# Down projection by Strassen's seven products for three of four pairs of token tiles

## The chip, the cores and the metric

The kernel runs on one core of a Trainium2 chip. A core has TensorE (PE, matrix products), VectorE (DVE), ScalarE (ACT), GpSimd (POOL) and SyncE (SP, which here only issues transfers). Each engine works through its own queue in order; semaphores hold an instruction until what it needs is there. The metric is the time of one execution on the device in microseconds (us). Before the change the median of three runs is 322.97 us (322.59 to 323.91).

## The reference

The input is x, 1024 tokens of width 512; everything is float32.

```
xn  = layernorm(x)
s   = silu(xn @ w_gate.T)                     # 1024 x 1376
s   = s with the 688 smallest |s| of each row set to 0
s   = s * (xn @ w_up.T)
ffn = routed experts (top 2 of 16, grouped) + shared expert, on xn
out = x + (s @ w_down.T) * silu(ffn)          # 1024 x 512
```

The change bears on the last line: the down projection `s @ w_down.T` (inner length 1376), the product with the gate `silu(ffn)`, the sum with x, and the store.

## The kernel before

**Tiles and pairs.** The 1024 tokens are eight tiles of 128. Tiles j and j+4 form pair j (`NP` = 4 pairs). `S[t]` is the tile's row of s, 128 x 1392 floats in SBUF. The gate and up projections and the experts' first layers are already done by Strassen's scheme with seven half-size products (class `Unit`, lines 652 to 700): products m1 to m7 are accumulated in three PSUM tiles, `al`, `be` and `de`; after m1, m6 and m5 ScalarE copies `al` to SBUF (`copy`, lines 658 to 661: m, u, v), and m6, m5, m3 go on adding to the same `al`. The four output quarters come from `de + m`, `al`, `be + v` and, after m4 is added to `be`, `be + u`. `weight_sums` (line 644) forms the sums of the weights' blocks, one subtraction for each of t1, t2, t4 and the new b12.

**Order.** The kernel is compiled with a manual schedule: the order in which the Python code issues instructions is the order on each engine's queue. A main loop over slots (lines 1341 to 1352) issues the products of gate, shared experts, up and routed experts. Between them a `Filler` (line 1136) issues the steps of the search for each row's threshold, one generator for each pair (`search`, line 820, before it `absolute`, line 811). One search makes five rounds of two counts on ScalarE (line 841) and seven small POOL operations (lines 852 to 858); then for each of its two tiles a last count, a masking of the row (line 866) and a maximum of eight (line 869) on VectorE; then nine small VectorE operations (lines 871 to 888) and for each tile one that drops the small values in `S[t]` (line 892). At the end of the main loop, pairs 0 and 1 have been through the search, pair 2 has done four of its five rounds, pair 3 two.

**The last stage** (from line 1354) is where the change is made. Tiles are handled in the order 0, 4, 1, 5, 2, 6, 3, 7 (`tiles`).

- `experts_base(i)` (line 1316): VectorE writes the biases of the experts for tile i into `y[t]`, two operations of 512 elements. `place` is the list of buffers for y; before, three lie in a retired weight buffer and three in the buffers t1, t2, t4 (`more_y`).
- `experts(i)` (line 1326, `experts_out` line 1088): TensorE makes three products into three PSUM tiles (`pys`, `pyr` twice); VectorE adds each to y (lines 1095, 1099); at the end ScalarE applies silu (line 1101), which gives the gate. After each of the three, the filler may be asked for steps.
- `turn_product(t, sT)` (line 1104): TensorE transposes the eleven chunks of `S[t]` (the last is 96 wide) in three groups, each with its own PSUM tile; ScalarE copies them to `sT` (lines 1113, 1119).
- `finish` (line 1121): eleven matmuls of width 512, `sT` against `wd_sb`, accumulate in one PSUM tile `po`; VectorE multiplies by the gate (line 1130), POOL adds x (line 1132), SP issues the store (line 1133). The last tile is done in two halves of 256 columns, with VectorE for the sum.

Before, the order is: experts of the first four tiles, turning of the first, and then for each tile the turning of the next, finish, and the experts of the tile four ahead.

**PSUM and SBUF.** All PSUM tiles come from one pool with one tag and eight banks (line 516); a new tile gets a bank whose former tile has been read. `wd_sb` is loaded at the end of the main loop into the buffer that the up weights leave (line 1355). The tiles of x are loaded a second time (`again`, four buffers).

Of the kernel before, what the change touches and what calls it, by code (L numbers as in the profile page):

```python
# [9 lines left out]
F32 = mybir.dt.float32  # L10
# [43 lines left out]
PERIOD = 7  # L54

# [434 lines left out]
def quick_path(  # L490
# [597 lines left out]
    def experts_out(t, g, ex):  # L1088
        def down_expert(name, which):
            py = psum(f"py{name}{t}")  # L1090
            mul_acc(py, [(h[:, ts(t, P)], w) for w, h in which], True)
            return py

        py = down_expert("s", ex[:2])
        nc.vector.tensor_add(g, g, py)
        yield
        for j, (gs, b3r) in enumerate(mix):
            py = down_expert(f"r{j}", ex[2 + j : 3 + j])
            nc.vector.scalar_tensor_tensor(g, py, gs[:, t : t + 1], g, ALU.mult, ALU.add)
            yield  # L1100
        nc.scalar.activation(g, g, AF.Silu)
# [19 lines left out]
    def finish(t, g, sT, xt, pieces=1):  # L1121
        for k in range(pieces):
            cols = ts(k, H // pieces)
            po = psum(f"po{t}_{k}")[:, : H // pieces]
            terms = []
            for c in range(IC):
                w = min(P, I - c * P)
                terms.append((sT[:w, c, :], wd_sb[:w, c, cols]))
            mul_acc(po, terms, True)
            nc.vector.tensor_mul(g[:, cols], po, g[:, cols])  # L1130
            add = nc.gpsimd if pieces == 1 else nc.vector
            add.tensor_tensor(g[:, cols], g[:, cols], xt[:, cols], ALU.add)  # L1132
            nc.sync.dma_start(out[ts(t, P), cols], g[:, cols])
# [92 lines left out]
    routed, hid, w3, b3s, du = [], [], [], [], {}  # L1226
# [66 lines left out]
    def fetch_w3():  # L1293
        w = w12("w3")
        for i in range(SLOTS):
            w3.append(w[:, ts(i, H)])
            fetch(w3[2 + i], w_rows, slots[i][0])
        b3s.append(w[:, 2 * H : 3 * H])
        nc.sync.dma_start(b3s[0], b3[E].partition_broadcast(P))
# [6 lines left out]
    ahead = 4  # L1306
# [5 lines left out]
    def more_y():  # L1312
        for k in ("t1", "t2", "t4"):
            place.append(big.tile([P, GW], F32, tag=k, name=f"{k}y")[:, :H])

    def experts_base(i):
        t = tiles[i]
        y[t] = place[i % 6]
# [9 lines left out]

    at(r_at + 20, begin_y)
# [3 lines left out]

    def search_job(j):
        yield from absolute(j)
        yield from search(j)

# [16 lines left out]
    more_y()  # L1354
    wd_sb = big.tile([P, IC * H], F32, tag="wB", name="wd_sb").rearrange("p (c n) -> p c n", c=IC)
    full = I // P
    for c0, c1 in ((0, 4), (4, 8), (8, full)):
# [3 lines left out]
    nc.sync.dma_start(wd_sb[: I - full * P, full, :], wd[full * P :, :])  # L1361
# [3 lines left out]
        for i in range(5)  # L1365
    ]
    for i in range(ahead):
        for _ in experts(i):
            filler.draw(0.3)
        if i + 3 < 6:  # L1370
            experts_base(i + 3)
    turn_product(tiles[0], sT[0])
    for i, t in enumerate(tiles):
        if i + 1 < NT:
            turn_product(tiles[i + 1], sT[(i + 1) % len(sT)])
        if i + 3 < NT:
            again[tiles[i + 3]] = load_x(tiles[i + 3], "r")
        finish(t, y[t], sT[i % len(sT)], again[t], pieces=2 if i == NT - 1 else 1)
        if i + ahead < NT:
            for _ in experts(i + ahead):  # L1380
                filler.draw(3)
            if i + 6 < NT:
                experts_base(i + 6)

        if i == NT - 4:
            filler.rest()
            worst = small.tile([P, 1], F32, tag="worst", name="worst")
            nc.vector.tensor_reduce(worst, bad, AX.X, ALU.add)
        if i == NT - 2:
            pf = psum("pf")  # L1390
            nc.tensor.matmul(pf[:1, :1], worst, ones[:, 0:1], start=True, stop=True)
            nc.vector.tensor_single_scalar(flag[:1, :], pf[:1, :1], 0.0, ALU.is_gt)

# [88 lines left out]
```

## Time and profile before

| | |
|---|---|
| median of three runs | 322.97 us (322.59 to 323.91) |
| the profiled execution's own time | 322.64 us |
| its span, from the first to the last recorded instruction | 320.8 us |
| granted TensorE clock, mean | 0.992 of full speed |
| `po` (down projection) on TensorE | 198 records, 77.1 us busy |
| line 841 (counts) on ScalarE | 40 + 8 records of 1.44 us |
| last stage on TensorE | from 200.5 to 314.7 us |

How to read what is shown further on. The busy table gives, for each engine, busy time, share of the span and number of instructions; PEld is the loading of a matmul's stationary operand, which overlaps PE. A line of a timeline gives the start, the duration, the engine, the source line, the operation, output<-inputs, the shape and the number of instructions merged; in brackets stands the idle time ahead of it and who ended it. Matmuls are pipelined and their ends are modelled, so starts are surer than ends. The line number 704 is that of the helper that issues all matmuls of a product; the PSUM tile's name tells which it is. A line of the chain gives start, duration, and what the end of the kernel was waiting for then. A line of the table by stretches gives from:to, its length, the busy time of PE, PEld, DVE, ACT and POOL, each with a count, then PEclk (granted TensorE clock as a share of full speed), the DMA engines' share and GB/s.

### The profile page before, as it was taken

How to read it: one execution, taken by the hardware profiler on the slowest of the kernel's cores; microseconds unless marked ns; L12 is line 12 of the kernel's file. 1: busy time of each engine (PE TensorE's matmuls, PEld its weight loads, DVE VectorE, ACT ScalarE, POOL GpSimd, SP SyncE). 2: the span in 40 equal slices, each digit the busy share in tenths (PEclk: the TensorE clock that was granted, in tenths of full speed). 3: DMA queues.
4: the chain of work that ended last, by engine and by line, in shares of the span. 5: the costliest groups of instructions: out<-in, count | busy, mean ns of one | idle time of the engine just before them, and what ended most of it. 6: DMA issues, size and time to landing. Idle time of an engine off the chain costs nothing.

```text
span 320.8 us, 3076 instructions
## 1 busy us (share of the span) xinstructions
PE 306.3 (95%) x964; PEld 172.8 (54%) x964; DVE 178.8 (56%) x384; ACT 148.4 (46%) x248; POOL 105.2 (33%) x229
## 2 busy tenths in 40 slices
PE   7899999999999997999999997999999999999992
PEld 3566566666544564654456664454545454555481
DVE  5988943323488671499399642790357889100011
ACT  2224556662983853637767567535181432211000
POOL 3242110112395078815532766400404020011010
PEclk9999999999999999799999999999999999999999
DMA  7992000000100006000070000910201020200010
GB/s 212 372 415 109 0 0 0 2 1 0 66 0 3 0 3 185 8 0 0 4 194 1 1 3 0 337 47 0 67 0 65 0 65 0 67 33 0 33 54 22
DMA packets 9735, 19.01 MB, mean 59 GB/s; under 512 B 1376, under 2 KB 3728, under 8 KB 9712
## 3 DMA queue, kind: packets, MB, share of 16 engines
q1 hardware_dynamic: 8976, 16.62, 15.2%
q0 software_dynamic: 736, 2.13, 2.5%
q8 instruction: 9, 0.15, 0.2%
q14 instruction: 14, 0.11, 0.1%
HBM read 16.65 MB, written 2.10 MB: 58 GB/s over the span
## 4 chain that ended last, share of the span: by engine, by line
PE 75%; DVE 10%; POOL 4%; ACT 4%; issue 2%; DMA 2%; SPq 0%; DVEq 0%; POOLq 0%
PE po L704 24%; PE palg L704 8%; PE palu L704 7%; PE pz L704 5%; PE pals L704 4%; PE pbeg L704 4%; PE pbeu L704 3%; PE palr L704 3%; PE pyr L704 3%; PE pys L704 3%; DMA wg_sb<-in_wg_dram 2%; PE ps L1111 2%; PE pdeg L704 2%; PE pbes L704 2%; ACT j L841 2%
## 5 line engine op out<-in xcount | busy, mean ns | idle before, releaser
L704 PE MATMUL po<-wd_sb,sT 128*128 128x512 f32 (+3 forms) x198 | 77.1, 546 | 0.7 <-ACT sT L1113 0.7
L841 ACT ACTIVATE j<-a,c 128x1376 bf16<-128x1376 f32 x40 | 57.7, 1443 | 24.4 <-POOL c L858 22.4
L704 PEld LDWEIGHTS po<-wd_sb,sT 128*128 128x128 f32 (+1 forms) x198 | 37.0, 190 | 35.6 <-issue 33.5
L704 PE MATMUL palu<-wu_sb,xs 128*128 128x344 f32 x64 | 22.4, 474 | 1.8 <-ACT vu L660 1.8
L1130 DVE TENSOR_TENSOR w_y<-po,w_y 128x512 f32<-128x512 f32 (+1 forms) x6 | 3.6, 602 | 33.6 <-PE po L704 33.6
L1132 POOL TENSOR_TENSOR w_y<-w_y,xr 128x512 f32<-128x512 f32 x4 | 5.1, 1268 | 51.0 <-DVE w_y L1130 41.6
L704 PE MATMUL pz<-wg_sb,xs 128*128 128x348 f32 x64 | 19.9, 461 | 1.4 <-ACT xs L630 0.9
L1113 ACT COPY sT<-ps 128x512 f32<-128x512 f32 (+1 forms) x24 | 10.7, 518 | 16.8 <-PE ps L1111 16.8
L1035 POOL TENSOR_TENSOR s<-s,vu 128x344 f32<-128x344 f32 x8 | 10.0, 1250 | 24.8 <-DVE vu L1034 24.7
L704 PEld LDWEIGHTS palu<-wu_sb,xs 128*128 128x128 f32 x64 | 12.7, 199 | 9.5 <-ACT vu L660 2.3
L704 PEld LDWEIGHTS pz<-wg_sb,xs 128*128 128x128 f32 x64 | 11.8, 190 | 8.2 <-ACT xs L630 1.5
L704 PE MATMUL palg<-wg_sb,xs 128*128 128x348 f32 x48 | 16.0, 456 | 0.0
L866 DVE SCALAR_TENSOR_TENSOR w<-a,c 128x1376 f32<-128x1376 f32 x8 | 13.8, 1722 | 2.3 <-POOL c L858 2.3
L704 PE MATMUL pys<-moe 128*128 128x512 f32 x32 | 15.0, 592 | 0.0
L704 PE MATMUL pyr<-w_w,moe 128*128 128x512 f32 x32 | 15.0, 592 | 0.0
L704 PE MATMUL palr<-xs,w_r 128*128 128x512 f32 x32 | 14.7, 592 | 0.0
L704 PE MATMUL pals<-xs,w_s 128*128 128x512 f32 x32 | 14.7, 592 | 0.0
L841 ACT ACTIVATE jc<-a,c 128x1376 bf16<-128x1376 f32 x8 | 11.5, 1443 | 4.9 <-POOL c L858 4.7
L892 DVE SCALAR_TENSOR_TENSOR s<-a,thr,s 128x1376 f32<-128x1376 f32 x8 | 13.1, 1644 | 0.0
L704 PE MATMUL palu<-t1u,xs 128*128 128x344 f32 x32 | 11.2, 474 | 1.9 <-ACT uu L660 1.9
L869 DVE MAX8 v<-w 128x8 f32<-128x1376 f32 x8 | 12.8, 1595 | 0.3
L1111 PEld LDWEIGHTS ps<-ident,s 128*128 128x128 f32 (+1 forms) x88 | 9.9, 139 | 3.7 <-issue 2.7
(230 smaller groups left out, 546.4 us busy)
## 6 DMA issues: line engine op xcount, KB each, us to landing
wu_sb<-in_wu_dram SPq DMA_DIRECT2D x4, 688.0 KB, 9.2
wg_sb<-in_wg_dram SPq DMA_DIRECT2D x3, 696.0 KB, 7.4
x<-in_x_dram SPq DMA_DIRECT2D x8, 256.0 KB, 4.0
xr<-in_x_dram SPq DMA_DIRECT2D x8, 256.0 KB, 4.6
wd_sb<-in_wd_dram SPq DMA_DIRECT2D x2, 1024.0 KB, 6.6
w_s<-in_wexp_dram SPq DMA_DIRECT2D x2, 512.0 KB, 5.4
out_dram<-w_y SPq DMA_DIRECT2D x4, 256.0 KB, 2.1
wg_sb<-in_wg_dram SPq DMA_DIRECT2D x1, 664.0 KB, 9.5
```

The lines of the kernel that those rows point to most:

```text
L704: nc.tensor.matmul(acc, a, b, start=first and i == 0, stop=i == len(terms) - 1, skip_group_check=not first,)
L841: nc.scalar.activation(junk, a[i], AF.Sign, bias=c[:, i : i + 1], scale=-1.0, accum_out=to[:, i : i + 1])
L866: nc.vector.scalar_tensor_tensor(w, a[i], c[:, i : i + 1], a[i], ALU.is_lt, ALU.mult)
L869: nc.vector.max(v[:, i, :], w)
L892: nc.vector.scalar_tensor_tensor(s, a[i], thr[:, i : i + 1], s, ALU.is_gt, ALU.mult)
L1035: nc.gpsimd.tensor_tensor(s, s, part, ALU.mult)
L1111: nc.tensor.transpose(pt[:w, ts(c - c0, P)], s[:, c * P : c * P + w], ident)
L1113: nc.scalar.copy(sT[:, c0 : c0 + full, :], pt[:, : full * P].rearrange("p (c n) -> p c n", c=full),)
L1130: nc.vector.tensor_mul(g[:, cols], po, g[:, cols])
L1132: add.tensor_tensor(g[:, cols], g[:, cols], xt[:, cols], ALU.add)
```

## The change

Pair 0 keeps `finish` for each of its two tiles, now without halves. Pairs 1, 2 and 3 go through a new class `Down(Unit)`: the two tiles' turned rows are a 2 x 2 block matrix (two tiles by two groups of `CH` = 5 chunks), the weights another (two groups of five chunks by two halves of 256 columns), and seven products of five matmuls of width 256 take the place of two times eleven of width 512. The last 96 rows of the inner length are added as one more matmul in each of m7, m2, m3 and m4; m4's takes the difference of the two halves of the weights' rows (`xw["diff"]`).

- The weights' sums t1, t2, t4 and the difference are formed by POOL after the turning of tile 0; b12, which pair 0 still needs in its old form, is replaced by VectorE after the second finish.
- The four sums of the rows (`sums`) are formed by VectorE in the buffers `S[j]` and `S[j + NP]` of the pair, which are free once turned.
- Each output quarter is `acc * g + (part * g + x)`: POOL prepares `part * g + x`, VectorE multiplies and adds, SP stores 128 x 256. The quarter out12 has no part, its second term is x.
- y's buffers are three of before, then four halves in `S[0]` and `S[4]`, then the first again. ScalarE's silu is no longer in `experts_out` but in `gate_of`.
- The order of the last stage is written out; the filler's steps are asked for by `some(n)`, and `turn_pair(j)` makes sure that pair j's search is complete.

```diff
+CH = 5
+LAST = I % P
             nc.vector.scalar_tensor_tensor(g, py, gs[:, t : t + 1], g, ALU.mult, ALU.add)
             yield
-        nc.scalar.activation(g, g, AF.Silu)
+    def finish(t, g, sT, xt):
+        po = psum(f"po{t}")
+        terms = []
+        for c in range(IC):
+            w = min(P, I - c * P)
+            terms.append((sT[:w, c, :], wd_sb[:w, c, :]))
+        mul_acc(po, terms, True)
+        nc.vector.tensor_mul(g, po, g)
+        nc.gpsimd.tensor_tensor(g, g, xt, ALU.add)
+        nc.sync.dma_start(out[ts(t, P), :], g)
+    class Down(Unit):
+        n = H // 2
+        def __init__(self, j, sT, gs, xts):
+            self.name, self.j, self.g, self.x = f"d{j}", j, gs, xts
+            top, bot = sT
+            s, k = S[j], CH * P
+            self.a = {
+                A11: top[:, :CH, :], A12: top[:, CH : 2 * CH, :],
+                A21: bot[:, :CH, :], A22: bot[:, CH : 2 * CH, :],
+            }
+            for blk, v in ((S1, S[j][:, :k]), (S2, S[j][:, k : 2 * k]), (S4, S[j + NP][:, :k])):
+                self.a[blk] = v.rearrange("p (c n) -> p c n", c=CH)
+            self.xtop, self.xbot = (v[:LAST, 2 * CH, :] for v in sT)
+        def sums(self):
+            a = self.a
+            nc.vector.tensor_add(a[S1], a[A21], a[A22])
+            nc.vector.tensor_sub(a[S2], a[S1], a[A11])
+            nc.vector.tensor_sub(a[A21], a[A11], a[A21])
+            nc.vector.tensor_sub(a[S4], a[A12], a[S2])
+        def mm(self, acc, blk, key, first, extra=()):
+            terms = [(self.a[blk][:, c, :], dd[key][:, c, :]) for c in range(CH)]
+            mul_acc(acc, terms + list(extra), first)
+        def m7(self):
+            self.be = self.acc("be")
+            self.mm(self.be, S3, "b12", True, [(self.xbot, xw["right"])])
+        def m2(self):
+            self.de = self.acc("de")
+            self.mm(self.de, A12, "b21", True, [(self.xtop, xw["left"])])
+            self.out11()
+        def m3(self):
+            self.mm(self.al, S4, "b22", False, [(self.xtop, xw["right"])])
+            self.out12()
+        def m4(self):
+            self.mm(self.be, A22, "t4", False, [(self.xbot, xw["diff"])])
+            self.out21()
+        def prepare_part(self, i, cols, part):
+            nc.gpsimd.tensor_tensor(part, part, self.g[i][:, cols], ALU.mult)
+            nc.gpsimd.tensor_tensor(part, part, self.x[i][:, cols], ALU.add)
+        def give(self, i, k, acc, part):
+            t, cols = self.j + NP * i, ts(k, H // 2)
+            g = self.g[i][:, cols]
+            nc.vector.tensor_mul(g, acc, g)
+            nc.vector.tensor_add(g, g, part)
+            nc.sync.dma_start(out[ts(t, P), cols], g)
+        def out11(self):
+            self.prepare_part(0, ts(0, H // 2), self.m)
+            self.give(0, 0, self.de, self.m)
+        def out12(self):
+            self.give(0, 1, self.al, self.x[0][:, H // 2 :])
+        def out22(self):
+            self.prepare_part(1, ts(1, H // 2), self.v)
+            self.give(1, 1, self.be, self.v)
+        def out21(self):
+            self.prepare_part(1, ts(0, H // 2), self.u)
+            self.give(1, 0, self.be, self.u)
...
-    def more_y():
-        for k in ("t1", "t2", "t4"):
-            place.append(big.tile([P, GW], F32, tag=k, name=f"{k}y")[:, :H])
...
+    def gate_of(i):
+        nc.scalar.activation(y[tiles[i]], y[tiles[i]], AF.Silu)
...
+    half = H // 2
+    dd = {
+        "b11": wd_sb[:, :CH, :half], "b12": wd_sb[:, :CH, half:],
+        "b21": wd_sb[:, CH : 2 * CH, :half], "b22": wd_sb[:, CH : 2 * CH, half:],
+    }
+    for k in ("t1", "t2", "t4"):
+        dd[k] = big.tile([P, GW], F32, tag=k, name=f"{k}d")[:, : CH * half].rearrange(
+            "p (c n) -> p c n", c=CH
+        )
+    xw = {"left": wd_sb[:LAST, full, :half], "right": wd_sb[:LAST, full, half:]}
+    xw["diff"] = spare[0][:LAST, :]
     flat = big.tile([P, 7, 2, HALF], F32, tag="xs", name="sT").rearrange("p b c n -> p (b c n)")
     sT = [
         flat[:, i * IC * P : (i + 1) * IC * P].rearrange("p (c n) -> p c n", c=IC)
-        for i in range(5)
+        for i in range(4)
     ]
-    for i in range(ahead):
+    def turn_pair(j):
+        while j not in found:
+            filler.one()
+        return [lambda k=k: turn_product(j + NP * k, sT[2 * (j % 2) + k]) for k in range(2)]
+    def unit_for(j):
+        return Down(
+            j, [sT[2 * (j % 2) + k] for k in range(2)],
+            [y[j + NP * k] for k in range(2)], [again[j + NP * k] for k in range(2)],
+        )
+    def some(n):
+        for _ in range(n):
+            filler.one()
+    for i in range(3):
         for _ in experts(i):
-            filler.draw(0.3)
-        if i + 3 < 6:
-            experts_base(i + 3)
-    turn_product(tiles[0], sT[0])
-    for i, t in enumerate(tiles):
-        if i + 1 < NT:
-            turn_product(tiles[i + 1], sT[(i + 1) % len(sT)])
-        if i + 3 < NT:
-            again[tiles[i + 3]] = load_x(tiles[i + 3], "r")
-        finish(t, y[t], sT[i % len(sT)], again[t], pieces=2 if i == NT - 1 else 1)
-        if i + ahead < NT:
-            for _ in experts(i + ahead):
-                filler.draw(3)
-            if i + 6 < NT:
-                experts_base(i + 6)
-        if i == NT - 4:
-            filler.rest()
-            worst = small.tile([P, 1], F32, tag="worst", name="worst")
-            nc.vector.tensor_reduce(worst, bad, AX.X, ALU.add)
-        if i == NT - 2:
+            some(1)
+        gate_of(i)
+    first = turn_pair(0)
+    first[0]()
+    weight_sums(G, *(dd[k] for k in KEYS), upto=3)
+    G.tensor_sub(xw["diff"], xw["left"], xw["right"])
+    place += [S[0][:, :H], S[0][:, H : 2 * H]]
+    experts_base(3)
+    some(4)
+    first[1]()
+    some(4)
+    place += [S[NP][:, :H], S[NP][:, H : 2 * H], place[0]]
+    finish(tiles[0], y[tiles[0]], sT[0], again[tiles[0]])
+    again[tiles[3]] = load_x(tiles[3], "r")
+    for _ in experts(3):
+        some(1)
+    for turn_one in turn_pair(1):
+        turn_one()
+    gate_of(3)
+    unit = unit_for(1)
+    unit.sums()
+    some(4)
+    finish(tiles[1], y[tiles[1]], sT[1], again[tiles[1]])
+    weight_sums(V, *(dd[k] for k in KEYS), since=3)
+    experts_base(4)
+    for j in range(1, NP):
+        more = j + 1 < NP
+        u, e = unit, 2 * j + 2
+        u.m1()
+        u.m7()
+        if j > 1:
+            gate_of(e - 1)
+        if more:
+            for i in (e, e + 1):
+                again[tiles[i]] = load_x(tiles[i], "r")
+        u.m6()
+        if more:
+            for _ in experts(e):
+                some(1)
+            experts_base(e + 1)
+            turns = turn_pair(j + 1)
+            turns[0]()
+            gate_of(e)
+        u.m2()
+        some(1)
+        u.m5()
+        if more:
+            some(1)
+            turns[1]()
+        else:
             pf = psum("pf")
             nc.tensor.matmul(pf[:1, :1], worst, ones[:, 0:1], start=True, stop=True)
             nc.vector.tensor_single_scalar(flag[:1, :], pf[:1, :1], 0.0, ALU.is_gt)
+        u.c22()
+        u.m3()
+        if more:
+            unit = unit_for(j + 1)
+            unit.sums()
+            for _ in experts(e + 1):
+                some(2)
+            if e + 2 < NT:
+                experts_base(e + 2)
+            else:
+                filler.rest()
+                worst = small.tile([P, 1], F32, tag="worst", name="worst")
+                nc.vector.tensor_reduce(worst, bad, AX.X, ALU.add)
+        u.m4()
```

## The prediction

> **What bounds the kernel now.** I read three views first: the busy table, TensorE's timeline from 200 us on, and the end of the chain that ended last.
>
> ```profile
> PE 306.3 (95%) x964; PEld 172.8 (54%) x964; DVE 178.8 (56%) x384; ACT 148.4 (46%) x248; POOL 105.2 (33%) x229
> ```
>
> ```profile
> 214.26 2.57 PE L1111 MATMUL ps<-ident,s 128*128 128x128 f32 x22
> 217.52 9.71 PE L704 MATMUL po<-wd_sb,sT 128*128 128x512 f32 x22 [0.69 <-ACT sT L1113]
> 227.07 1.88 PE L704 MATMUL pys<-moe 128*128 128x512 f32 x4
> 228.79 1.88 PE L704 MATMUL pyr<-w_w,moe 128*128 128x512 f32 x4
> 230.51 1.36 PE L1111 MATMUL ps<-ident,s 128*128 128x128 f32 x11
> 231.71 9.61 PE L704 MATMUL po<-wd_sb,sT 128*128 128x512 f32 x22
> ...
> 304.91 9.77 PE L704 MATMUL po<-wd_sb,sT 128*128 128x256 f32 x44
> ```
>
> ```profile
> 304.98 9.71 PE po L704 x44
> 314.69 0.02 issue
> 314.72 0.44 DVE w_y L1130
> ```
>
> TensorE sets the end: from 200.5 to 314.69 us it stands still only 0.69 us, ahead of the first down product. Starts give the prices, since an end overlaps the next start: a down product costs 9.45 us (231.71 to 241.16), the expert products of a tile 3.44 (227.07 to 230.51), the turning of a tile 1.20. An f32 matmul has two records here. At width 512 one record takes 9.45/22 = 0.43 us; at width 256, from the chain, 9.71 less 0.17 for the last one's way out, over 44: 0.217 us. Half the width is half the price. After TensorE's end come 0.44 + 0.42 us of VectorE and 5.2 us of the last store and the close.
>
> **What TensorE saves.** A pair had two down products, 18.90 us. It now has seven products of five chunks at width 256, 35 matmuls, and four matmuls for the 96 last rows: 39 x 2 x 0.217 = 16.9 us. Three pairs save 6.0. The 0.69 us ahead of the first down product goes: that wait came from ScalarE's gate of the fourth tile (line 1101), and experts(3) now comes after finish. TensorE's list without waits, from 200.53: three experts 10.30, two turnings 2.40, finish 9.45, experts 3.44, two turnings 2.40, finish 9.45, three pairs 50.8, four experts 13.75, four turnings 4.80, the flag's matmul 0.12, last way out 0.17. It ends at 307.6: **7.1 us** less.
>
> **What is added elsewhere, without waits.** POOL: three subtractions of 1280 elements. 344 elements take 0.915 us (line 1035) and 688 take 1.65 (line 647), so 2.14 ns each and 0.18 once: 2.92 us each, and 0.73 for "diff". VectorE: one such subtraction for b12 and four of 640 elements a pair. Its line 647 takes 0.42 us at 256 and 0.88 at 696: 1.48 and 0.82 us. The output quarters are two VectorE operations of 0.42 each (the last store's row) where one of 0.69 stood, and mostly two POOL operations of 0.73 where one of 1.27 stood. Three ScalarE copies a pair, some 0.4 each by line 660, lie under other products. Twelve stores of 128 KB replace seven of 256 KB and two halves, on SP's queue; 128 KB lands in 2.1 us, and an x load there is needed 10 us later. The filler's steps are only moved: three were issued in the first three experts, now nine, then eight more before the first finish.
>
> **Where this meets a wait: VectorE and POOL.** The page shows VectorE at 56%, but not what POOL does to it. The timelines of the two around 92 us do:
>
> ```profile
> 93.06 0.51 DVE L937 TENSOR_TENSOR sc<-sc,sm 128x128 f32<-128x128 f32 x1
> 93.60 1.70 DVE L938 TENSOR_TENSOR sc<-sc,rbias_sb 128x128 f32<-128x128 f32 x1
> ...
> 95.88 0.97 DVE L910 TENSOR_TENSOR prg<-gm,tmg 128x32 f32<-128x32 f32 x1
> ```
>
> ```profile
> 91.77 1.65 POOL L647 TENSOR_TENSOR t2u<-wu_sb,t1u 128x688 f32<-128x688 f32 x1
> 93.50 1.65 POOL L647 TENSOR_TENSOR t4u<-wu_sb,t2u 128x688 f32<-128x688 f32 x1
> 95.11 1.69 POOL L647 TENSOR_TENSOR wu_sb<-wu_sb 128x688 f32<-128x688 f32 x1
> ```
>
> Each VectorE operation with two operands in SBUF ends some 0.1 us after the POOL operation that ran when it came: 93.57, 95.30, 96.85 after 93.42, 95.15, 96.80. A 128-element operation needs about 0.3, so it stood still for the rest; and between 93.42 and 93.57 POOL's next waited for it. They take turns, a whole operation each. Operations with one operand in PSUM are untouched (0.68 at 90.11).
>
> Follow that from 211.6. The nine filler steps put four counts on ScalarE (line 841, 1.56 us each, one after another from 202.5, with the first gate's 0.5 between), and POOL's update of tile pair 2's threshold (seven small operations, 2.0) needs the fourth, done at 209.6. So POOL starts t1 at 211.6; VectorE is through with the third tile's experts at 211.7 and wants experts_base(3). By turns, each hand-over saving 0.15: t1 to 214.6, base to 215.2, t2 to 217.9, base to 218.5, t4 to 221.3, the first masking (line 866, 1.65) to 222.8, its maximum (1.60, one operand) to 224.4, the second pair of these to 227.7, nine small ones (1.70) to 229.3, finish's multiply to 229.9, the add of experts(3) to 230.5, then line 892, held by POOL's add of x, to 232.7, and the scale of the first routed product to 233.4. Without POOL's three, all this would be 8.5 us earlier.
>
> Who waits? PSUM has eight banks under one tag. The three experts before finish run without a gap on TensorE although VectorE empties each only 0.7 us or more later, so a bank is not reused at once: I take the one that is free longest. From finish on come 1 bank, 3 (experts), 3 and 3 (turnings), 1 (second finish). Counting eight back, the second group of the second turning needs finish's bank, the third the expert's first, the second finish the expert's second. TensorE wants them at 227.8, 228.2 and 228.5 and gets them at 229.9, 230.5 and 233.4. **Stall 4.9 us.** If VectorE's base comes ahead of t1, a matter of 0.1 us, the same sum ends at 232.4: 3.9. I take 4.4; if the banks are free, 0.
>
> **The clock.** Two idle stretches of 1 to 2.4 us stand in that stall. The windows by stage show what such a stretch did at 125.4 to 127.3 us:
>
> ```profile
> 124.00:128.00 4.00, 2.09 (x7) 1.06 (x7) 0.52 (x1) 0.45 (x1) 3.67 (x5) 1.00 0.60 171
> 128.00:132.00 4.00, 4.00 (x9) 2.40 (x8) 0.52 (x1) 0.85 (x3) 3.09 (x14) 0.57 0.12 34
> ```
>
> After 1.91 us of idleness the granted clock is 0.57 (second column from PEclk's end, ahead of the DMA share) in the next 4 us: about 3.4 us at half speed, 1.7 lost. A gap of 1.75 at 196.4 cost nothing. The Trainium skill ("TensorE: Matmul & The Clock Gate", "Why this matters for your kernels") warns of "PE-idle gaps >~3µs". By that limit both stretches are free and the sum is 1.3 us better; the row says that 1.9 can be enough. (The free-running window of some 3.4 us in the page's Part 1 would fit both gaps, if half a window must be idle.) I follow the row: **1.3** (0 to 1.7).
>
> **Smaller waits.** m7 of the first pair needs b12, which VectorE may write only after the second finish: multiply 0.68 + 1.48 against m1's 2.17: **0.2**; 1.3 more if POOL's add takes its turn first. m4 of that pair overwrites the bank that out22's multiply reads. TensorE comes to m4 23.7 us after m1's start (five products 11.7, two of experts 6.9, two turnings 2.4, m3 2.6, b12 0.2). VectorE starts experts(4)'s add at 9.0 and has 14.6 us ahead of the end of that multiply: add and two scales 2.1, both maskings and maxima of tile pair 3 6.5, experts_base(5) 1.5, out11 0.8, nine small ones 1.7, line 892 1.6, itself 0.4; POOL's turns (out22's and out21's parts) add 1.0. That is 24.6: **0.9** (0 to 2). In the last pair nothing but the flag stands between m5 and m3, and m3 adds to the bank that ScalarE is copying; such a wait was 0.54 at 30.1 us: **0.5**. The four row sums end 4 us before the m7 that reads them; the "two operations instead of one" delay no bank. The tail stays as it is.
>
> **Sum.** -7.1 + 4.4 + 1.3 + 0.2 + 0.9 + 0.5 = +0.2 us on the span of 320.8. The profiled execution took 322.64, 1.84 more than its span; the median, 322.97, is 0.33 above it. The forecast is no change: **323.2 us**, its own range 320.8 to 325.3, since stall and clock are each open by 1 us or more, the m4 wait by 1.
>
> **Rivals.** (1) The banks are free in time: the allocator gives the turnings banks that ScalarE has just emptied, or VectorE is earlier than I count. Then stall and clock go: -7.1 + 1.6 = -5.5, 317.5 us. For it: in the profile before, no bank is ever waited for, so the order of reuse is inferred only. Against: the turn-taking is seen three times over, and VectorE has 8.5 us less with only 6 us of cover. (2) In between: VectorE wins some turns or its queue is 2 to 3 us shorter, the stall is 1 to 2 us and the clock holds: 319.5. (3) Slower: POOL keeps the port over t1, t2, t4 and diff, since each follows at once. VectorE's 13.2 us and the 1.1 for POOL's add then begin at 221.1, the second finish at 235.4: stall 6.9, clock 1.5, sum +2.9, 325.9. It decides from a stall of 5.8 us on, other terms as they are. Against it stands 93.42, where POOL let VectorE in.
>
> **Chances.** Forecast 50, rival 1 28, rival 2 8, rival 3 14 in 100. Half a per cent is 1.6 us, about what a measurement can tell from no change. The forecast's own spread puts 11 of its 50 below that, 29 within, 10 above. So faster 0.47, same 0.29, slower 0.24. The range, 316.9 to 325.8, leaves out a part of rivals 1 and 3.
>
> **What would show it.** Right: in the second turning after the first finish and at the second finish TensorE is idle for 1 to 2.5 us each, released by VectorE (the multiply of finish, the experts' scale); VectorE's base and first masking, near 212 to 223 us, last 2 to 4 us each instead of 0.75 and 1.65; POOL's t1, t2, t4 take some 2.9 us, or 3.4 with VectorE's turn; a granted clock near 0.5 for some 3 us after; each pair's 78 records take 16.9 us without other gaps but 0.5 in the last. Wrong: TensorE without a gap from 200 us to the first pair (rival 1), or three POOL subtractions in a row with VectorE idle beside them (rival 3).

## The result and the profile after

The changed kernel takes **320.57 us** (median of 14 executions, 318.83 to 323.08) against 322.88 us for the kernel before (14, 321.81 to 324.95): a ratio of **0.9923, with a 95% interval of 0.9895 to 0.9952**. That is faster by 2.3 us, a little more than the half per cent that the prediction set as its bound, and not the "no change" that the prediction gave as its forecast (over all its cases, "faster" had 0.47 of its chances); the range held. Measured again beside the experiments it was 0.9943 (0.9915 to 0.997). The profiled execution took 319.98 us, 2.66 less than the one before; its span is 318.2 us instead of 320.8. In the changed kernel's source, lines up to about 1100 stand two further on than before (704 is now 706).

The busy table:

```profile
PE 300.4 (94%) x1044; PEld 187.1 (59%) x1044; DVE 205.6 (65%) x412; ACT 152.0 (48%) x257; POOL 127.8 (40%) x246
```

VectorE has 27 us more busy time, but not all of that is work: some 8 us are the length of operations that were held up (its busy time is 197.6 us in the first experiment, where POOL forms no sums), as its timeline shows below. First TensorE's timeline over the stretch where the prediction looked for its stall, then the places of the smaller waits and the end:

```profile
211.23 2.57 PE L1112 MATMUL ps<-ident,s 128*128 128x128 f32 x22
213.63 9.61 PE L706 MATMUL po<-wd_sb,sT 128*128 128x512 f32 x22
...
224.79 1.88 PE L706 MATMUL pyr<-w_w,moe 128*128 128x512 f32 x4
226.51 1.80 PE L1112 MATMUL ps<-ident,s 128*128 128x128 f32 x15
230.09 1.14 PE L1112 MATMUL ps<-ident,s 128*128 128x128 f32 x7 [1.78 <-DVE w_y L1129]
231.07 9.61 PE L706 MATMUL po<-wd_sb,sT 128*128 128x512 f32 x22
240.52 2.32 PE L706 MATMUL pald<-wd_sb,sT 128*128 128x256 f32 x10
242.95 2.83 PE L706 MATMUL pbed<-wd_sb,sT 128*128 128x256 f32 x12
...
262.68 1.88 PE L706 MATMUL pyr<-w_w,moe 128*128 128x512 f32 x4
265.28 2.43 PE L706 MATMUL pbed<-t4d,sT 128*128 128x256 f32 x10 [0.72 <-DVE s L1186]
...
305.86 0.19 PE L1519 MATMUL pf<-ones,worst 128*1 128x1 f32 x2
306.39 2.43 PE L706 MATMUL pald<-wd_sb,s 128*128 128x256 f32 x10 [0.34 <-ACT vd L662]
...
311.25 0.60 PE L706 MATMUL pbed<-w_w,sT 96*128 96x256 f32 x2
```

There is one idle stretch of 1.78 us and not two. It lies where the prediction put the first: after fifteen transposes (eleven of tile 1, four of tile 5) the next group needs a bank that finish's multiply (line 1129) has to read. The second finish, for which the prediction had the longest wait, starts at 231.07 right behind the last transposes.

VectorE and POOL beside it:

```profile
212.10 3.17 DVE L1387 SCALAR_TENSOR_TENSOR s<-b3r,gs,w_w 128x512 f32<-128x512 f32 x1
215.30 3.28 DVE L1387 SCALAR_TENSOR_TENSOR s<-b3r,gs,s 128x512 f32<-128x512 f32 x1
218.50 4.30 DVE L868 SCALAR_TENSOR_TENSOR w<-a,c 128x1376 f32<-128x1376 f32 x1
...
229.36 0.68 DVE L1129 TENSOR_TENSOR w_y<-po,w_y 128x512 f32<-128x512 f32 x1
...
230.55 2.29 DVE L894 SCALAR_TENSOR_TENSOR s<-a,thr,s 128x1376 f32<-128x1376 f32 x1
232.77 1.59 DVE L1101 SCALAR_TENSOR_TENSOR s<-pyr,gs,s 128x512 f32<-128x512 f32 x2
```

```profile
211.72 3.00 POOL L649 TENSOR_TENSOR t1d<-wd_sb 128x1280 f32<-128x1280 f32 x1
214.80 3.24 POOL L649 TENSOR_TENSOR t2d<-wd_sb,t1d 128x1280 f32<-128x1280 f32 x1
218.11 3.24 POOL L649 TENSOR_TENSOR t4d<-wd_sb,t2d 128x1280 f32<-128x1280 f32 x1
221.31 2.08 POOL L1472 TENSOR_TENSOR w_w<-wd_sb 96x256 f32<-96x256 f32 x1
```

The two gate bases (0.75 us each when alone) last 3.2 and 3.3, the masking (1.65 alone) 4.3. The bases end 0.55 us after POOL's t1 and t2, the masking 1.45 after t4, which is what each still needs once its turn comes; and POOL's t2 and t4 last 0.24 us longer than t1, which had no turn to wait for. The scale that frees the bank of the expert's second product starts only at 232.77, 1.7 us after the second finish began: that finish had no need of it.

The windows by stage; the clock is the third number from the end:

```profile
124.00:128.00 4.00, 2.79 (x10) 1.52 (x8) 0.52 (x1) 0.26 (x2) 3.37 (x4) 1.00 0.61 194
128.00:132.00 4.00, 3.33 (x12) 2.24 (x13) 0.52 (x1) 1.55 (x4) 3.42 (x12) 1.00 0.31 76
...
230.00:234.00 4.00, 3.90 (x14) 2.14 (x15) 3.90 (x5) 1.02 (x3) 1.28 (x1) 1.00 0.41 125
```

In this execution the clock stays at 1.00 behind the wait. Near its end, the chain that ended last goes through ScalarE's copy of v, for which the last m3 waits:

```profile
305.96 0.38 ACT vd L662
306.39 2.86 PE pald L706 x12
```

### The profile page after: what moved, and what is told of

Read it like the earlier page. It is cut to its first block, busy times and chain, and to the rows that moved or that the text cites. A ratio compares the mean times of both kernels' runs of the same rounds, so it can differ in the third digit from the quotient of the medians.

```text
span 318.2 us, 3328 instructions
## 1 busy us (share of the span) xinstructions
PE 300.4 (94%) x1044; PEld 187.1 (59%) x1044; DVE 205.6 (65%) x412; ACT 152.0 (48%) x257; POOL 127.8 (40%) x246
## 4 chain that ended last, share of the span: by engine, by line
PE 61%; DVE 20%; POOL 7%; issue 4%; ACT 3%; DMA 3%; SPq 0%; DVEq 0%; POOLq 0%
PE palg L706 8%; PE pald L706 7%; DVE w L868 5%; PE pbed L706 5%; PE pz L706 5%; PE pals L706 4%; PE pbeg L706 4%; DVE v L871 4%; PE palu L706 3%; PE pys L706 3%; PE pyr L706 3%; PE po L706 3%; DMA wg_sb<-in_wg_dram 3%; POOL s L1037 3%; DVE s L1387 2%
## 5 line engine op out<-in xcount | busy, mean ns | idle before, releaser
L706 PE MATMUL palu<-wu_sb,xs 128*128 128x344 f32 x64 | 21.2, 454 | 1.7 <-ACT vu L662 1.7
L1037 POOL TENSOR_TENSOR s<-s,vu 128x344 f32<-128x344 f32 x8 | 11.4, 1419 | 24.8 <-DVE vu L1036 24.7
L706 PE MATMUL po<-wd_sb,sT 128*128 128x512 f32 (+1 forms) x44 | 19.2, 592 | 0.0
L868 DVE SCALAR_TENSOR_TENSOR w<-a,c 128x1376 f32<-128x1376 f32 x8 | 16.5, 2061 | 0.7 <-POOL c L860 0.6
L854 POOL TENSOR_SCALAR d<-d 128x2 f32<-128x2 f32 x20 | 4.6, 232 | 29.5 <-ACT j L843 29.1
L706 PEld LDWEIGHTS po<-wd_sb,sT 128*128 128x128 f32 (+1 forms) x44 | 8.2, 190 | 9.6 <-issue 9.1
L894 DVE SCALAR_TENSOR_TENSOR s<-a,thr,s 128x1376 f32<-128x1376 f32 x8 | 13.8, 1726 | 0.0
L662 ACT COPY md<-pald 128x256 f32<-128x256 f32 x3 | 1.1, 374 | 26.0 <-PE pald L706 26.0
L1112 PE MATMUL ps<-ident,s 128*128 128x128 f32 (+1 forms) x88 | 11.0, 274 | 1.8 <-DVE w_y L1129 1.8
```

Source lines behind the costliest of these rows:

```text
L662: nc.scalar.copy(v, self.al)
L706: nc.tensor.matmul(acc, a, b, start=first and i == 0, stop=i == len(terms) - 1, skip_group_check=not first,)
L854: nc.gpsimd.tensor_scalar(d, d, 0.5, I / 2 - AIM, ALU.mult, ALU.add)
L868: nc.vector.scalar_tensor_tensor(w, a[i], c[:, i : i + 1], a[i], ALU.is_lt, ALU.mult)
L894: nc.vector.scalar_tensor_tensor(s, a[i], thr[:, i : i + 1], s, ALU.is_gt, ALU.mult)
L1037: nc.gpsimd.tensor_tensor(s, s, part, ALU.mult)
```

## The experiments

The theory after the result: VectorE is late because it takes turns with POOL's three sums; this alone makes TensorE's wait at 228 us, and that wait is what keeps the change from its full 5.5 us. Rivals: the wait comes from the number of VectorE's operations ahead of finish's multiply; or from the order in which PSUM banks are given out, whatever VectorE does; or the gain went elsewhere.

For comparing runs I use TensorE's **tail**, from the start of pair 0's turning (211.23 here) to the end of the last matmul (311.25 + 0.60). It leaves out what varies in the main loop. It is 100.62 us in the profile above.

### Without POOL's sums

```diff
-    for k in ("t1", "t2", "t4"):
-        dd[k] = big.tile([P, GW], F32, tag=k, name=f"{k}d")[:, : CH * half].rearrange(
-            "p (c n) -> p c n", c=CH
-        )
+    dd.update(t1=dd["b11"], t2=dd["b22"], t4=dd["b21"])
...
-    xw["diff"] = spare[0][:LAST, :]
+    xw["diff"] = xw["right"]
...
-    weight_sums(G, *(dd[k] for k in KEYS), upto=3)
-    G.tensor_sub(xw["diff"], xw["left"], xw["right"])
```

> Leaves out POOL's three sums of the weights and the difference: t1, t2, t4 are b11, b22, b21 themselves and the difference is the right half, so pairs 1 to 3 come out as other numbers; every matmul stays. Theory (POOL's sums hold the SBUF port that VectorE's two-operand operations need, which makes finish's multiply late, and a group of the second turning waits for its bank): experts_base after the first turning takes 0.75 us twice instead of 3.2, the first masking 1.65 instead of 4.3, finish's multiply comes before 224 us, and the 1.78 us wait of TensorE ahead of the last seven transposes is gone; the median is 1.8 to 2.6 us below the changed kernel's, about 318. Rival (VectorE's queue alone is too long, POOL does not matter): VectorE's durations and the wait stay, the time stays at 320.6.

Measured: 316.82 us (316.73 to 317.03), ratio to before 0.982 (0.9793 to 0.9846); tail 98.46. The two bases last 0.74 and 0.75 us, the masking 1.65, finish's multiply starts at 222.31 (this profile's tail starts 1.1 us earlier), and the 22 transposes of pair 1's turning are one line without a wait. VectorE's first base, then TensorE:

```profile
210.99 0.74 DVE L1387 SCALAR_TENSOR_TENSOR s<-b3r,gs,w_w 128x512 f32<-128x512 f32 x1
```

```profile
225.41 2.57 PE L1112 MATMUL ps<-ident,s 128*128 128x128 f32 x22
```

The waits of 0.72 and 0.34 us further on are unchanged. So the sums on POOL cost the kernel 2.16 us in the tail. The medians lie 3.75 us apart; where the rest comes from is the subject of the last experiments.

### The same sums on VectorE

```diff
-    weight_sums(G, *(dd[k] for k in KEYS), upto=3)
+    weight_sums(V, *(dd[k] for k in KEYS), upto=3)
```

> The three sums t1, t2, t4 are done by VectorE at the same place (POOL keeps the difference). VectorE gets 4.4 us more to do in its own queue. Theory (port): it loses 4.4 us instead of about 9, finish's multiply ends near 227 us, before TensorE asks for the bank at 228.3, no wait: 1.8 to 2.6 us below the changed kernel, about 318. Rival (queue length): 4.4 us more in front of the multiply, the wait grows from 1.8 to about 6 us and the time to 324 or more.

Measured: 317.59 us (316.69 to 317.85), ratio 0.9832 (0.9803 to 0.9862); tail 98.46, the same as without any sums. VectorE's timeline:

```profile
212.13 1.70 DVE L649 TENSOR_TENSOR t1d<-wd_sb 128x1280 f32<-128x1280 f32 x1
213.87 1.49 DVE L649 TENSOR_TENSOR t2d<-wd_sb,t1d 128x1280 f32<-128x1280 f32 x1
...
216.80 0.75 DVE L1387 SCALAR_TENSOR_TENSOR s<-b3r,gs,w_w 128x512 f32<-128x512 f32 x1
...
226.45 0.68 DVE L1129 TENSOR_TENSOR w_y<-po,w_y 128x512 f32<-128x512 f32 x1
```

TensorE's wait is gone here too:

```profile
226.54 2.56 PE L1112 MATMUL ps<-ident,s 128*128 128x128 f32 x22
```

More work on VectorE, and it is through 2.9 us earlier. On VectorE the three sums cost it 4.7 us; on POOL, where they were put to relieve it, they cost it 7.6 (0.75 + 0.75 + 1.65 became 3.17 + 3.28 + 4.30). The length of VectorE's list is refuted as the cause.

### Four steps of the search later

```diff
     first[1]()
-    some(4)
     place += [S[NP][:, :H], S[NP][:, H : 2 * H], place[0]]
```

> Only the second group of four filler steps (second masking and maximum, nine small operations, an update) is taken from between the second turning and the first finish; the steps that follow all come four later. POOL keeps its sums, so VectorE's long operations stay. Theory (the late multiply holds the bank): the multiply now stands ahead of the second masking and ends near 225 us, the wait ahead of the last seven transposes goes although VectorE is as slow as before; the searches of pair 3 move behind m3 of the first pair, so the 0.9 us ahead of m4 goes too: 2 to 3 us below the changed kernel, 317.5 to 318.5. Rival (the wait is for VectorE's total work, which is unchanged): a wait of the same size shows at the second finish or at m7, the time stays at 320.6.

Measured: 316.99 us (316.89 to 317.24), ratio 0.9824 (0.9798 to 0.9851); tail 98.41. POOL's sums are as before, and the bases (3.18, 3.28) and the masking (4.29) as long as ever, but finish's multiply now stands ahead of the second masking and starts at 223.33 (this profile's tail starts 1.0 us earlier). TensorE's timeline, with the new small wait at m7:

```profile
225.48 2.56 PE L1112 MATMUL ps<-ident,s 128*128 128x128 f32 x22
227.88 9.61 PE L706 MATMUL po<-wd_sb,sT 128*128 128x512 f32 x22
237.33 2.32 PE L706 MATMUL pald<-wd_sb,sT 128*128 128x256 f32 x10
240.03 2.83 PE L706 MATMUL pbed<-wd_sb,sT 128*128 128x256 f32 x12 [0.38 <-DVE wd_sb L649]
```

The turn-taking does no harm here once nothing that TensorE waits for is queued behind it. The steps taken out come back before the second finish and delay b12, on which m7 waits; at the same time m4's wait of 0.72 us is gone, and one of 0.24 appears in a later turning.

### The old kernel with the fourth expert moved

```diff
-    ahead = 4
+    ahead = 3
```

> The kernel before with one change, experts of three tiles instead of four ahead of the first down product: the part of the new order that takes the 0.69 us wait away, without the seven products. Theory: 0.7 us below the kernel before, about 322.2, the same 0.69 being all that TensorE stood still. Rival: the wait comes back somewhere else, 322.9.

Measured: 322.08 us (20 executions) beside 322.7 (23), ratio 0.9983 (0.9971 to 0.9994). The wait of 0.69 us became one of 0.38, and the time fell by 0.6:

```profile
213.60 9.71 PE L704 MATMUL po<-wd_sb,sT 128*128 128x512 f32 x22 [0.38 <-ACT sT L1113]
```

So this part of the change of order is by itself worth half a microsecond or so; the rest of the saving has to come from the products, whose records show it.

### POOL busy, but only writing

```diff
-    weight_sums(G, *(dd[k] for k in KEYS), upto=3)
+    for k in ("t1", "t2", "t4"):
+        for _ in range(3):
+            G.memset(dd[k], 0.0)
```

> The changed kernel with GpSimd's three sums of the weights replaced by nine fills (three for each sum): GpSimd stays busy beside VectorE for some microseconds, but only writes, so the products of the pairs that use the sums are not those of the reference. The difference row stays. Theory (VectorE is slowed because the other engine reads SBUF beside it): VectorE's gate-base operations fall from 3.2 us to about 0.75 each while the fills run, the masking from 4.3 to about 1.65 unless it meets the difference row; the finish's multiply starts at about 222.5 instead of 229.4, TensorE's 1.78 us wait in the second turning is gone; about 316.9 us, ratio to before about 0.982. Rival (any busy GpSimd instruction slows VectorE): the operations beside the fills stay at about 3 us as long as fills last, and the wait shrinks only by what the fills are shorter than the sums.

Measured: 316.94 us (316.66 to 318.14), ratio 0.9823 (0.9804 to 0.9843); tail 98.45. POOL's timeline, then VectorE's:

```profile
211.75 3.61 POOL L1473 MEMSET t1d<- 128x1280 f32 x3
...
218.86 3.61 POOL L1473 MEMSET t4d<- 128x1280 f32 x3
```

```profile
212.15 0.74 DVE L1387 SCALAR_TENSOR_TENSOR s<-b3r,gs,w_w 128x512 f32<-128x512 f32 x1
...
213.60 1.65 DVE L868 SCALAR_TENSOR_TENSOR w<-a,c 128x1376 f32<-128x1376 f32 x1
```

POOL is busy for 10.7 us on end beside VectorE, longer than with its three sums, and VectorE is not slowed at all. Pair 1's 22 transposes are again one line (226.56 to 229.12). What the engines take turns for is the reading of SBUF. The Trainium skill says this ("SBUF — State Buffer", "Who interferes with whom"): a VectorE instruction with two inputs in SBUF contends with a GpSimd instruction that reads SBUF, not with one that only writes it. The rows agree.

### The dose doubled

```diff
-    weight_sums(G, *(dd[k] for k in KEYS), upto=3)
+    for _ in range(2):
+        weight_sums(G, *(dd[k] for k in KEYS), upto=3)
```

> The changed kernel with GpSimd's three sums done twice over, the dose doubled. Theory (the shared port sets VectorE's lateness and that sets TensorE's wait): VectorE's operations up to the first masked search stay long for another 9 us or so, but there are only 18 us of them in all, so VectorE's t1 to the second masking stretch by 5 to 9 us; the finish's multiply comes at 234 to 238 instead of 229.4, TensorE's wait in the second turning grows from 1.8 to 7 to 10 us, and the run ends at 326 to 331 us, part of it a lower clock after the gap. Rival (a fixed wait, set by the bank's order and not by the sums): wait and time stay as they are, 320 to 321 us.

Measured: 326.44 us (two executions, 326.04 and 326.84), ratio 1.0121 (1.0095 to 1.0147). TensorE's timeline and the windows:

```profile
233.91 1.75 PE L1112 MATMUL ps<-ident,s 128*128 128x128 f32 x7 [6.66 <-DVE w_y L1129]
235.46 11.78 PE L706 MATMUL po<-wd_sb,sT 128*128 128x512 f32 x22
```

```profile
230.00:232.00 2.00, 0.00 (x0) 0.00 (x0) 1.94 (x2) 0.00 (x0) 2.00 (x2) 0.50 0.00 0
...
238.00:240.00 2.00, 2.00 (x4) 0.92 (x3) 2.00 (x3) 1.47 (x2) 0.00 (x0) 0.54 0.26 98
240.00:242.00 2.00, 2.00 (x6) 0.83 (x5) 1.90 (x4) 1.97 (x4) 0.00 (x0) 1.00 0.00 0
```

The wait grows from 1.78 to 6.66 us, just under what was expected, since in its second half VectorE's list holds fewer operations with two inputs in SBUF. The clock falls to a half in the middle of it, at 229.6, and stays there until 239.8: the last seven transposes and the finish last 2.8 us longer than in the changed kernel (1.75 and 11.78 for 1.14 and 9.61). The wait (4.9 us more) and the clock (2.8) together make the tail 7.6 us longer, 108.23 us. The medians are only 5.9 apart, which fits what the next experiments show: a slower clock behind the wait is part of the changed kernel's median too.

### The changed kernel again, and three more profiles of it

The kernel is the changed one, unaltered.

> The changed kernel itself once more, beside the others on the same chip, for the spread of its times and clocks. Theory (its 1.8 us wait at about 228 us costs its own length in every execution, and in some a stretch at a lower clock behind it): times between 319 and 323 us, the granted clock of the runs between 0.983 and 0.996 and the longer times at the lower clocks, about 0.25 us for 0.001; the versions without that wait do not go below 0.989. Rival (the spread is the chip's own and has nothing to do with the wait): the versions without the wait spread as widely, over 2 us, at clocks down to 0.984.

> The changed kernel once more, one profile, to see where an execution of it at a clock of 0.983 to 0.985 loses its 2.4 us against one at 0.991 to 0.997. Theory (the 1.8 us wait at 228 us is sometimes followed by a stretch at half the clock): if this execution comes out at 321.4 us or more, the granted clock falls from 1.0 to about 0.5 for some 3 to 5 us within 2 us behind the wait, the 22 transposes or the finish behind it last 2 to 3 us longer than 9.6 us, and nothing else differs by over 0.5 us; if it comes out below 320 us, the clock stays at 1.0 there. Rival (the loss is elsewhere, in the loop that the change leaves alone): the stretch behind the wait looks alike in both, and the main loop ends 2 us later.

> The same once more, as the outcome differs between executions: about one in two is expected at 321.4 us or above. Theory and rival as for the first look: half a clock for 3 to 5 us behind the wait with 2 to 3 us lost there, or a later end of the main loop.

> The same a third time. Theory and rival as for the first look: half a clock for 3 to 5 us behind the wait with 2 to 3 us lost there, or a later end of the main loop.

Measured: nine executions gave 319.06, 319.11, 319.33 and 319.64 us at a mean granted clock of 0.991 to 0.997, and 321.44, 321.51, 321.79, 321.93 and 321.95 at 0.983 to 0.985, with nothing between. The three further profiles, A, B and C, came out at 321.96 (clock 0.983), 319.06 (0.996) and 319.5 (0.995). Profile A's timeline and windows, then B's windows:

```profile
230.07 1.43 PE L1112 MATMUL ps<-ident,s 128*128 128x128 f32 x7 [1.77 <-DVE w_y L1129]
231.29 11.06 PE L706 MATMUL po<-wd_sb,sT 128*128 128x512 f32 x22
```

```profile
128.00:132.00 4.00, 4.00 (x9) 2.40 (x9) 0.52 (x1) 0.45 (x1) 3.17 (x14) 0.57 0.25 51
...
230.00:234.00 4.00, 3.93 (x11) 2.20 (x12) 3.90 (x5) 1.12 (x3) 1.27 (x1) 0.60 0.21 74
```

```profile
230.00:234.00 4.00, 4.00 (x12) 1.85 (x11) 3.90 (x4) 1.41 (x5) 0.32 (x1) 1.00 0.38 135
```

The wait is nearly the same in both, 1.77 and 1.80 us. In A the clock then falls to a half, and its tail is 102.30 us against 100.64, 1.7 us lost behind a wait of 1.8. The rival holds for the rest: A also has a half-clock stretch at 128 to 132, and it takes 73.2 us instead of 72.3 from the end of the gap before it (127.72; 127.54 in B) to the first expert (200.91; 199.84). The main loop's gap is in both kernels; only the second loss belongs to the change.

Of the changed kernel's 26 executions, ten have a clock of 0.985 or less and none of these took under 321.4 us. Of the 21 executions of the five versions without the wait (no sums, sums on VectorE, steps later, fills, and the one that follows) none is below 0.989, and none took over 318.2 us. Taken at like clocks, the difference shrinks: ten executions of the changed kernel at 0.994 to 0.997 have a median of 319.2 us, the four without sums, at 0.993 to 0.998, one of 316.8. That is 2.35 us, near the 2.16 of the tail. The rest of the 3.75 goes, by the clocks, to half-clock stretches, of which the four without sums had none in the main loop either; with four executions that can be luck.

### A better version

Both moves of the steps, and the last pair's order changed, so that the last m3 finds the copy done:

```diff
     first[1]()
-    some(4)
...
     unit.sums()
-    some(4)
+    some(2)
     finish(tiles[1], y[tiles[1]], sT[1], again[tiles[1]])
     weight_sums(V, *(dd[k] for k in KEYS), since=3)
+    some(2)
...
+        if not more:
+            for _ in experts(e - 1):
+                some(2)
...
+            u.m6()
...
-        u.m6()
...
+        if not more:
+            u.m5()
...
```

In the last pair the products now come in the order m1, the experts of tile 7, m6, m7, m5, m2, the flag, m3, m4.

> The changed kernel without the four steps of the search ahead of the second finish (as e3_late), with two of the four steps behind it moved behind VectorE's subtraction for b12, and the last pair's order changed: the experts of the last tile are taken before the fourth product of the pair ahead, in the last pair they stand between its first and its sixth product, and m7 and m5 go further back. Theory (each short wait left in the list is worth its own length): e3_late's 317.0 less m7's 0.38 us and less the last m3's wait of 0.34 us: about 316.2 us, ratio to before 0.980; TensorE's list without a wait over 0.3 us except before the fourth product of the first pair. Rival (waits of this size are hidden, or the new order makes as many new ones): 316.8 to 317.3 us.

Measured: 316.75 us (316.43 to 317.36), ratio 0.9817 (0.9801 to 0.9834); tail 97.72. m4's wait is gone, m7's is back at the 0.3 us of the changed kernel, 0.24 us remain in a turning, and the last m3 follows the flag's product at once:

```profile
303.79 0.19 PE L1528 MATMUL pf<-ones,worst 128*1 128x1 f32 x2
303.90 2.42 PE L706 MATMUL pald<-wd_sb,s 128*128 128x256 f32 x10
```

The tail is 0.7 us shorter than that of the version with four steps moved, as was forecast. In the median it can't be told from the version with four steps moved (316.99), and the profiled execution's main loop happened to hold a half-clock stretch. It beats both kernels, as do the two simpler edits above.

## Why the prediction was right and wrong

The terms of its sum, against TensorE's starts from the first expert on (200.53 before, 200.93 after; 114.16 us before, 110.92 after). Waits are taken from start to start, so they hold the way out of the last matmul as well and come out above the bracketed idle times.

| term | forecast, us | profiled execution, us |
|---|---|---|
| list without waits | -7.1 | -7.0 |
| stall at second turning and second finish | +4.4 | +2.2 |
| m7 waits for b12 | +0.2 | +0.3 |
| m4 of the first pair | +0.9 | +0.9 |
| last pair's m3 | +0.5 | +0.4 |
| clock behind the stall | +1.3 | 0 here; 1.7 in profile A |
| start of the stretch and tail | 0 | +0.4 and +0.2 |
| sum | +0.2 | -2.6 |

How the measured ones are worked out: start of pair 1's turning to second finish 231.07 - 226.51 = 4.56 against 2.40; m1 to m7 2.43 against 2.16 in the next pair; the expert's product to m4 2.60 against 1.72; flag to m3 0.53 against 0.11 in the better version. What is left of 110.92 is 107.2 us. The +0.4 is scatter of the main loop: in the five profiles of the changed kernel the first expert starts between 199.84 and 200.93.

**The savings were right.** Half the width is half the price, and 39 x 2 x 0.217 us a pair is what the records show. The three smaller waits, each worked out from single operations ahead, are right to 0.1 us. For m4's, whose own range was 0 to 2, so close a hit is luck.

**The turn-taking was right**, in mechanism and size. The walk had the two bases end at 215.2 and 218.5, the masking at 222.8, finish's multiply at 229.9; measured are 215.3, 218.6, 222.8 and 230.0. The fills and the sums on VectorE show that it is this and nothing else that makes VectorE late. Only its total of 8.5 us was too high: the three held operations lost 7.6, and without the sums finish's multiply comes 5.9 us earlier in the tail, since VectorE then waits 1.57 us for one of ScalarE's counts.

**The step that failed** is "Counting eight back, the second group of the second turning needs finish's bank, the third the expert's first, the second finish the expert's second." The first part holds: TensorE stands before that group until the multiply. The last does not: the second finish began at 231.07, with the expert's second bank still to be read at 232.77. The program as compiled gives the banks out so, in TensorE's order:

| PSUM tiles | banks |
|---|---|
| first finish | 4 |
| three experts of tile 5 | 3, 7, 1 |
| turning of tile 1, three groups | 5, 6, 2 |
| turning of tile 5, three groups | 0, 4, 3 |
| second finish | 5 |

Up to the turning of tile 5 this is the rotation by eight that the prediction supposed from the kernel before, and there, in the last stage, it holds throughout. The second finish would then get bank 7, the expert's second. It gets bank 5, that of the first group of tile 1's turning, which ScalarE copied out of 3.4 us earlier:

```profile
227.15 1.35 ACT L1114 COPY sT<-ps 128x512 f32<-128x512 f32 x3 [5.47 <-PE ps L1112]
```

So the stall is 2.2 us and not 4.4, and the second idle stretch does not occur. An estimate from the rows: with bank 7 the second finish would have had to wait for the first of the two scales at 232.77 (0.8 us each), until 233.5, and the stall would have been 4.6 us. No run here changed the banks alone. But the versions with no sums, sums on VectorE, steps later, fills, doubled sums and the better version all have the banks of this table, and TensorE's wait is there 0, 0, 0, 0, 6.66 and 0 us: the banks say what TensorE waits for, VectorE's lateness whether and how long. That refutes the rival of the bank order "whatever VectorE does". Why the compiler leaves the rotation at this one tile is open.

The number is that of rival 2 (a stall of 1 to 2 us and a clock that holds, 319.5 us), which got 8 chances in 100; the profiled execution is within 0.5 us of it. Its reason is not: VectorE won no turns and was as late as forecast. What happened is nearer to the reason of rival 1, a bank that ScalarE had just emptied, for this one tile only.

**The clock term** was mis-shaped. It was booked as a fixed 1.3 us for two idle stretches; for the one that is there it is nothing in some executions and 1.7 us in others (by their clocks, at least ten of 26). The 1.7 us that the prediction drew from the row at 128 us was the right price here, though in the main loop such a stretch cost only 0.9 (73.2 for 72.3). This, with the main loop's stretch, is why the median, 320.57, lies between 319 and 322, and why taking the wait away gains more in the median than in the tail. The limit of 3 us that the Trainium skill names ("TensorE: Matmul & The Clock Gate", "Why this matters for your kernels") would have given no loss behind a wait of 1.77 us; profile A shows one.

**Rival 1's number was right for another kernel**: with stall and clock gone, it said 317.5; the five versions where they are gone took 316.75 to 317.59.

## What to carry to other kernels

Work given to POOL was not free for VectorE where it read SBUF: look at which VectorE operations with two SBUF inputs run beside it and who on TensorE waits for what is queued behind them. A bank freed late matters only to the tile that is given that bank, so a forecast that rests on the order of banks should be read from the compiled program or be carried as two cases. A wait of TensorE of nearly 2 us can cost twice its length, in some executions only (1.77 us and 1.7 more in profile A, 1.80 and nothing more in B); one profile of a kernel need not show it.

## What the runs showed of the hardware that was not expected

- **A half clock behind gaps of less than 2 us, in some executions only.** Over thirteen profiles, the main loop's gap of 1.88 to 1.92 us was followed by a clock of 0.57 to 0.59 at 128 to 132 us in five and by 1.00 in eight. The gap of 1.73 to 1.76 near 197 us never was. The wait of 1.77 to 1.83 us at 228 was in one of five profiles of the changed kernel.
- **The half clock comes in whole periods of 3.41 us, on a fixed beat.** Each of the six short stretches, five in the main loop and one at 230, lasts 3.41 us; behind the gap of 6.66 us it lasts three of them, 10.24, from 229.6 to 239.8. They begin 2.3 to 2.8 us after the idle time began, which is after work was resumed where the gap is short. In profile A the two begin at 128.39 and 230.79, 102.40 us apart, thirty periods. The Trainium skill describes a free-running window of about 3.4 us ("TensorE: Matmul & The Clock Gate", "Part 1: The HAM clock gate"); these figures agree with it.
- **Where a gap falls on this beat differs between executions.** I count periods from the first full clock that each profile records, 4 to 8 us into the span. The main loop's gap then lies whole within one period in all five profiles with the half clock. In six of the eight without, a period's edge cuts it; in the other two it starts within 0.05 us of an edge, too near to tell. So its chance is largely this phase. Length counts too: the gap of 1.73 to 1.76 us lay whole within one period in eight profiles and cost nothing, so half a period of idleness (1.71), which the prediction's parenthesis supposed, is not enough here. It is not the whole account: the wait at 228 us lay whole within one in four of five profiles, and only the shortest of these, 1.77, was followed by the half clock; why is open.
- **The mean clock of an execution counts these stretches.** 3.4 us at half speed in a span of 318 is 0.0053. The changed kernel's executions lie at 0.994 to 0.997, 0.989 to 0.991 and 0.983 to 0.985; B and C, without a stretch, had 0.996 and 0.995, A, with two, 0.983. The rest is a half clock after the last matmul, in every profile (from 314.56 us to the end in the changed kernel's first one), which costs TensorE nothing.
- **Nine fills of 1280 elements take 1.2 us each on POOL** and leave VectorE alone, where subtractions of the same size take 2.9 to 3.0 each and hold up the VectorE operations beside them that read two operands in SBUF. With the sums doubled, one operation with a single input was held too: line 873, 0.15 us elsewhere, took 1.24 and ended with POOL's second t2.
